# Attention over a graph's edges on one Trainium2 core: the edges' biases summed inside the keys' rows instead of added afterwards

## The chip, the core and the metric

The kernel runs on one core of one Trainium2 chip. The metric is the device time of one execution in microseconds. TensorE is called PE in what follows (its weight loads PEld), VectorE DVE, ScalarE ACT, GpSimd POOL, SyncE SP. Before the change six runs have a median of 11079.71 us (11026.39 to 11104.98).

## What is computed

Two layers of a graph network over 10,000 nodes of 512 numbers and 160,000 edges (src, dst), sorted by dst. The first layer is a mixture of four two-layer graph convolutions. The second, which the change touches, is attention along the edges with 8 heads of 64, a feed-forward part and norms:

```python
z = _layernorm(x, ln_att_g, ln_att_b)
q = (z @ Wq.T + bq).reshape(n, H, D)
k = (z @ Wk.T + bk).reshape(n, H, D)
v = (z @ Wv.T + bv).reshape(n, H, D)
s = jnp.einsum('ehd,ehd->eh', q[src], k[dst]) / np.sqrt(D) + att_bias
m = jax.ops.segment_max(s, src, num_segments=n)
p = jnp.exp(s - m[src])
denom = jax.ops.segment_sum(p, src, num_segments=n)
alpha = p / jnp.where(denom[src] == 0, 1.0, denom[src])
agg = jax.ops.segment_sum(alpha[:, :, None] * v[dst], src, num_segments=n)
att = agg.reshape(n, C) @ Wo.T + bo
x = x + att
z = _layernorm(x, ln_ff_g, ln_ff_b)
h = jax.nn.silu(z @ W1.T + b1)
x = x + h @ W2.T + b2
```

`att_bias` has 8 numbers for each edge, one for each head. They are the biases that the change moves.

## The kernel before

The work has three stages. The first two compute the first layer; at the end of the second, `nodes(b)` computes q, k and v of a block of 128 nodes and writes k and v side by side into rows of `kv_all`: 512 numbers of k, then 8 heads of 65 numbers of v, whose 65th place holds a one, so that the weighted sum of the v rows gives the denominator too (`VH` = 65, `KVW` = 512 + 520 = 1032).

The third stage is the attention with its feed-forward part. The 79 blocks of 128 source nodes are cut into windows of 32 nodes, 4 a block, 316 in all. A window's edges fill five chunks of 128 edges, one edge a partition. Four chunks are the window's own and lie in one of four buffers `kvb`; the fifth is shared by the four windows of a block and lies in one of three buffers `kvo`. POOL fetches the rows of `kv_all` by index (`fetch`, L1797), two windows ahead. Indices, places and biases of a block's edges are in a tile `meta`.

All order is written out by hand, on PE, DVE, ACT and POOL: each engine runs its instructions in the order in which the program lists them. The loop `for w in range(NW + 3)` is one window, j is its place in the block. Within it:

- `score(g)` (L2071, DVE) multiplies the queries, spread to the edges by PE (`expand`, L2034), with two chunks of keys, in place; after both, L2107 sums 64 products a head, and L2110 adds the biases from `meta`. The shared chunk goes the same way once a block, at j = 3: `expand_over` (L2042), `score_over` (L2048, L2050, L2052). Its result is copied into the window's scores by ACT at the head of the window (L2065).
- `weigh(w, s)` is a generator that three windows in a row drive on: maxima (L1936), turned by PE into a PSUM tile `turns` (L1938), the top (L1941), spread back by PE (L1943), subtracted (L1945), exp (L1948), a one-hot matrix times the weights (L1957: chunks 2 to 4 on POOL, 0 and 1 on DVE), 80 small products on PE (L1971), denominators (L1976, L1977), the scaled sums (L1980), turned (L1982) and copied into `att_t` (L1983).
- The one-hot matrices of a block's edges are made by DVE at the end of j = 1 (`open_block`, L1772, L1776, copied twice by ACT, L1778). PE turns four of them for each window two windows ahead (`turn_hots`), and the four of the shared chunk (`over_t`) at the end of j = 2; both through `turned` (L1821, L1824), whose PSUM place is in the same bank as the turned maxima.
- The feed-forward part of blocks already done is cut into small pieces. `front(b)` projects the attention's result (L1839, L1841), adds the input (L1845), norms (L1848, L1918, L1921, L1924, L1925, L1851) and turns it (L1862, L1863); `back` computes the two layers for two blocks together (L1879, Silu L1881; L1889, L1891); `tail` adds and norms the result (L1897, L1901, L1904). They are generators too. A piece that yields a positive cost is PE work and runs when credit is there; a `yield 0` puts the rest off to the next call. `advance(rate)` is called four times a window:

```python
credit[0] = min(credit[0], 0.5) + rate
for job in list(jobs):
    free = True
    while job.cost not in (None, STOP) and (
            free if job.cost == 0 else rate and credit[0] >= 0.5 * job.cost):
        free = free and job.cost > 0
```

A job thus passes at most one `yield 0` in a call. The calls are at the head of the window (rate 2.6), before the second products (0), before the next turning of one-hots (0), and before L2107 (2.4). `front(b)` is made at j = 2 of the next block, just ahead of the last of these.

Of the kernel before, what the change touches and what calls it, by code (L numbers as in the profile page):

```python
# [13 lines left out]
ALU = mybir.AluOpType  # L14
# [5 lines left out]
D = 512  # L20
# [3 lines left out]
H = 8  # L24
# [592 lines left out]
FAR = 999.0  # L617
WP = 2 + H
VH = DH + 1
KVW = D + H * VH  # L620

GROUP = 5
ROWS_OF = {1: P, 2: 2 * P, 3: 2 * P, 4: 3 * P, 5: 3 * P}
# [14 lines left out]
def fast(ctx: ExitStack, tc: tile.TileContext, a: dict, out: bass.AP, bad: bass.AP):  # L638
# [112 lines left out]
    def normed(pool, src, t):  # L751
        st = pool.tile([P, 6], F32, name="st")
        nc.vector.bn_stats(st, src)
        mv = pool.tile([P, 2], F32, name="mv")
        nc.vector.bn_aggr(mv, st)
        rs = pool.tile([P, 2], F32, name="rs")
        nc.scalar.activation(rs[:, 0:1], mv[:, 1:2], AF.Sqrt, bias=eps)
        nc.vector.reciprocal(rs[:, 0:1], rs[:, 0:1])
        nc.vector.scalar_tensor_tensor(rs[:, 1:2], mv[:, 0:1], -1.0, rs[:, 0:1],
                                       op0=ALU.mult, op1=ALU.mult)  # L760
        nc.scalar.activation(t, src, AF.Identity, scale=rs[:, 0:1], bias=rs[:, 1:2])
        return t

    mid = ExitStack()
    mp = mid.enter_context(tc.tile_pool(name="mid", bufs=1))
# [677 lines left out]
    with ExitStack() as p2:  # L1443
# [178 lines left out]
        def nodes(b):  # L1622

            xb = load_x(dp, b, 1)
            for v in range(2):
                nc.gpsimd.indirect_dma_start(
                    out=back[:, v, :], out_offset=None,
                    in_=done_s[group[b] % 3][:NE * GR[group[b]], :],
                    in_offset=row_at(pos_i[:, v, b:b + 1]),
                    bounds_check=NE * GR[group[b]] - 1, oob_is_err=False)  # L1630
            yield
            for v in range(2):
                nc.vector.scalar_tensor_tensor(xb, back[:, v, :], gsel[:, v, b:b + 1], xb,
                                               op0=ALU.mult, op1=ALU.add)
            x1 = normed(dp, xb, back[:, 0, :])
            nc.sync.dma_start(x1_all[b * P:(b + 1) * P, :], x1)
            z = normed(dp, x1, back[:, 1, :])
            yield
            pt = pt_.tile([P, KD, P], F32, name="pt")
            for k in range(KD):  # L1640
                nc.tensor.transpose(pt[:, k, :], z[:, k * P:(k + 1) * P], ident)
            z_t = dp.tile([P, KD, P], F32, name="z_t", bufs=1)
            nc.scalar.copy(z_t, pt)  # L1643
            yield
            r = slice(b * P, (b + 1) * P)
            for i in (1, 2, 0):
                po = pm.tile([P, D], F32, name="mm")
                for k in range(KD):
                    nc.tensor.matmul(po, z_t[:, k, :], wqkv[i][:, k, :], start=(k == 0),  # L1649
                                     stop=(k == KD - 1))  # L1650
                row = bias[:, NE + i, :]
                if i == 1:
                    nc.vector.tensor_add(kv[:, :D], po, row)
                elif i == 2:
                    nc.vector.tensor_add(kv[:, D:].rearrange("p (h d) -> p h d", h=H)[:, :, :DH],
                                         po.rearrange("p (h d) -> p h d", h=H),
                                         row.rearrange("p (h d) -> p h d", h=H))
                    nc.sync.dma_start(kv_all[r, :], kv)
                else:

                    q3 = dp.tile([P, 3, D], BF16, name="q3", bufs=1)
                    left = dp.tile([P, D], F32, name="left", bufs=1)
                    s = DH ** -0.5
                    nc.vector.tensor_add(left, po, row)
                    nc.scalar.activation(q3[:, 0, :], left, AF.Copy, scale=s)
                    nc.vector.scalar_tensor_tensor(left, left, s, q3[:, 0, :],
                                                   op0=ALU.mult, op1=ALU.subtract)
                    nc.scalar.copy(q3[:, 1, :], left)
                    nc.vector.tensor_sub(q3[:, 2, :], left, q3[:, 1, :])
                    nc.sync.dma_start(q_all[b].rearrange("t p d -> p t d"), q3)  # L1670
                yield
# [34 lines left out]
    with ExitStack() as p3:  # L1706
# [125 lines left out]
        def front(b):  # L1832

            x1, att_t = rest.pop(b)
            bank = yield from take()
            po = banks[bank]
            for h in range(NQ):
                yield WO
                nc.tensor.matmul(po, att_t[:, h, :, :].rearrange("p j n -> p (j n)"), wo[:, h, :],  # L1839
                                 start=(h == 0), stop=False)  # L1840
            nc.tensor.matmul(po, onesb, bias[:, 0, :], start=False, stop=True)  # L1841
            yield 0
            yield 0
            x2 = dp.tile([P, D], F32, name="x2", bufs=4)
            nc.vector.tensor_add(x2, po, x1)  # L1845
            yield 0
            st = dp.tile([P, 6], F32, name="st")
            nc.vector.bn_stats(st, x2)  # L1848
            rs, mean = yield from scale(st)
            z = dp.tile([P, D], F32, name="z")  # L1850
            nc.scalar.activation(z, x2, AF.Identity, scale=rs, bias=mean)  # L1851
            nc.gpsimd.tensor_tensor(x2, x2, x1, op=ALU.add)
            yield 0
            yield 0
            yield TURN
            i = b % 2
            if i == 0:
                pairs[b // 2] = z_ts[b // 2 % 2], []
            z_t, mine = pairs[b // 2]
            pt = po.rearrange("p (k n) -> p k n", n=P)  # L1860
            for k in range(KD):
                nc.tensor.transpose(pt[:, k, :], z[:, k * P:(k + 1) * P], ident)  # L1862
            nc.scalar.copy(z_t[:, :, i * P:(i + 1) * P], pt)  # L1863
            unused.append(bank)
            mine.append((b, x2))
            if i or b == NB - 1:
                jobs.append(Job(back(*pairs.pop(b // 2))))
# [42 lines left out]
        def take():  # L1910
            while not unused:
                yield 0
            return unused.pop(0)
# [16 lines left out]
        def weigh(w, s):  # L1930
# [35 lines left out]
            for c in range(CAP):  # L1966
                kv = kvb[w % KB][:, c, :] if c < SC_W else kvo[b % 3]
                for f in range(2):
                    for h in range(4):
                        v = D + (f * 4 + h) * VH  # L1970
                        nc.tensor.matmul(acc[h * W:(h + 1) * W, f, :], ohp[:, c, f * 4 + h, :],  # L1971
                                         kv[:, v:v + VH], start=(c == 0 and f == 0),
                                         stop=(c == CAP - 1 and f == 1), skip_group_check=True)
# [37 lines left out]
        with tc.manual_schedule(engines={ET.PE, ET.DVE, ET.Activation, ET.Pool}):  # L2011
# [32 lines left out]

            def score_over(b):
                if b < NB:
                    k = kvo[b % 3][:, :D]
                    nc.vector.tensor_tensor(k, qe.pop(b)[:, 0, :], k, op=ALU.mult)  # L2048
                    s = s_over[b] = dp.tile([P, H], F32, name="s_over")
                    nc.vector.tensor_reduce(s, k.rearrange("p (h d) -> p h d", h=H),  # L2050
                                            axis=AX.X, op=ALU.add)
                    nc.vector.tensor_add(s, s, blocks[b][0][:, SBC - 1, 2:])  # L2052

            expand_over(0)
            score_over(0)
            expand(0, 0)
            expand(0, 1)
            EARLY, LATE = 2.6, 2.4
            for w in range(NW + 3):
# [3 lines left out]
                if w < NW:  # L2063
                    s = dp.tile([P, CAP, H], F32, name="s", bufs=3)
                    nc.scalar.copy(s[:, SC_W, :], s_over[b])  # L2065

                def score(g):
                    if w < NW:
                        cs = GROUPS[g]
                        k = kv[:, cs[0]:cs[-1] + 1, :D]  # L2070
                        nc.vector.tensor_tensor(k, qe.pop((w, g)), k, op=ALU.mult)  # L2071

# [25 lines left out]
                if last:  # L2100
                    expand(w + 1, 1)
                advance(LATE)
                if j == 2 and b + 1 < NB:
                    over_t[b + 1] = turned(b + 1, range(SC_W, BC, CAP), "over_t", 2)
                first = iter(())
                if w < NW:
                    nc.vector.tensor_reduce(s[:, :SC_W, :],  # L2107
                                            kv[:, :, :D].rearrange("p c (h d) -> p c h d", h=H),
                                            axis=AX.X, op=ALU.add)
                    nc.vector.tensor_add(s[:, :SC_W, :], s[:, :SC_W, :],  # L2110
                                         blocks[b][0][:, j * SC_W:(j + 1) * SC_W, 2:])
                    first = weigh(w, s)
                    next(first)
                next(first, 1)
# [65 lines left out]
```

## Time and profile before

| | us |
|---|---|
| median of six runs | 11079.71 |
| profiled execution | 11096.67 |
| its span, first to last instruction | 11094.9 |
| PE busy over the span | 9407.8 (85%) |
| DVE busy | 5185.0 (47%) |
| ACT busy | 2975.6 (27%) |
| POOL busy | 7004.7 (63%) |
| mean granted clock of PE | 0.932 |

The averages over the span hide the stages. From 8000 to 11000 us, all of it in the third stage, PE is busy for 2615 of 3000 us, DVE for 2509, ACT for 1837 and POOL for 1966; the DMA engines' mean share is 0.76, at 243 GB/s.

A line of a group gives the source line, engine and operation, the tiles written and read, shapes and count, then busy us and mean ns of one, then the engine's idle time just before these instructions, with what ended it. A line of the timeline gives start and duration in us, and in brackets the idle time before. The chain of waits follows back, from the last instruction, what each one waited for.

### The profile page before, as it was taken

What the parts mean: (1) busy time and instruction counts of PE and PEld (TensorE: products, weight loads), DVE (VectorE), ACT (ScalarE), POOL (GpSimd) and SP (SyncE); (2) the same over time, 40 slices, a digit from 0 to 9 for tenths busy, and PEclk for the clock granted to TensorE, in tenths of its full rate; (3) what the DMA queues carried; (4) which work ended last, traced back from release to release, by engine and by line L of the source; (5) the groups of instructions that cost most, each with busy time, mean ns of one, the idle gap of its engine ahead of it and who ended that gap; (6) DMA issues with size and microseconds to landing.
All of it is one profiled execution on the core that took longest, in us unless ns stands there. A gap on an engine that the chain in (4) does not pass through costs nothing. (4 is left out here: it accounts for less than half of the span.)

```text
span 11094.9 us, 154933 instructions
## 1 busy us (share of the span) xinstructions
PE 9407.8 (85%) x56450; PEld 4520.8 (41%) x56450; DVE 5185.0 (47%) x8694; ACT 2975.6 (27%) x5619; POOL 7004.7 (63%) x6861
## 2 busy tenths in 40 slices
PE   7999999999986777887878888888788888888888
PEld 2443444333331222333333333333455555555555
DVE  5888884111130111221222222222588888888885
ACT  1110111011000111111111111112256666666665
POOL 5566676666657766666666666664366666666664
PEclk8999999999998888999889999999899999999999
DMA  8555555555546666776767777775577777777774
GB/s 253 171 163 166 161 171 168 157 161 169 157 136 208 211 217 208 241 238 222 234 222 239 241 242 239 236 229 170 174 244 248 248 243 244 247 251 246 246 243 131
DMA packets 931577, 2328.72 MB, mean 210 GB/s; under 512 B 202864, under 2 KB 288758, under 8 KB 930806
## 3 DMA queue, kind: packets, MB, share of 16 engines
q0 software_dynamic: 575968, 1787.05, 51.0%
q1 hardware_dynamic: 344864, 518.29, 14.1%
q10 hardware_dynamic: 9974, 13.39, 0.4%
q8 instruction: 449, 7.36, 0.3%
q14 instruction: 322, 2.64, 0.1%
HBM read 2047.01 MB, written 394.25 MB: 220 GB/s over the span
## 5 line engine op out<-in xcount | busy, mean ns | idle before, releaser
L1269 POOL DMA_INDIRECT ring<-in_x_dram,idx_t x1264 | 1634.9, 1293 | 887.0 <-PE p_ag L1305 466.2
L1344 PE MATMUL mm<-big,tt 128*128 128x512 f32 x4424 | 2025.5, 609 | 32.3 <-issue 17.6
L1141 POOL DMA_INDIRECT sorted<-pay,addr x1250 | 1267.2, 1014 | 381.0 <-issue 355.0
L1344 PEld LDWEIGHTS mm<-big,tt 128*128 128x128 f32 x4424 | 841.3, 195 | 1158.1 <-issue 1100.7
L1599 PE MATMUL mm<-big,turned 128*128 128x512 f32 x2688 | 1236.8, 603 | 1.4 <-issue 1.3
L1504 POOL DMA_INDIRECT ring<-h_tab,ix x747 | 763.4, 1022 | 620.1 <-PE p_ag L1539 180.9
L1797 POOL DMA_INDIRECT kv<-kv_all,meta x948 | 981.3, 1035 | 256.4 <-issue 201.8
L1649 PE MATMUL mm<-ext,z_t 128*128 128x512 f32 x1896 | 915.4, 634 | 190.4 <-ACT z_t L1643 117.1
L1348 ACT ACTIVATE y<-y 128x512 f32<-128x512 f32 x316 | 198.9, 629 | 2801.1 <-DVE y L1347 2274.3
L1504 POOL DMA_INDIRECT y<-h_tab,ix x596 | 608.6, 1021 | 510.7 <-issue 156.4
L1957 POOL TENSOR_TENSOR ohp<-oh,p 128x768 f32<-128x768 bf16 x316 | 467.0, 1478 | 694.2 <-ACT p L1948 694.2
L1539 PE MATMUL p_ag<-ring,oh 128*32 128x512 f32 x2812 | 723.7, 645 | 184.5 <-DMA ring<-h_tab,ix 141.9
L1347 DVE TENSOR_TENSOR y<-mm,bl 128x512 f32<-128x512 f32 x316 | 216.8, 688 | 1323.2 <-PE mm L1344 428.5
L1539 PE MATMUL p_ag<-y,oh 128*32 128x512 f32 x2244 | 623.4, 648 | 174.5 <-DMA y<-h_tab,ix 130.1
L1602 DVE TENSOR_TENSOR res<-mm,bias 128x512 f32<-128x512 f32 x192 | 132.7, 691 | 1332.8 <-PE mm L1599 646.8
L1879 PE MATMUL bank<-big,big 128*128 128x256 f32 (+1 forms) x2560 | 632.2, 391 | 86.2 <-ACT big L1881 78.3
L1599 PEld LDWEIGHTS mm<-big,turned 128*128 128x128 f32 x2688 | 496.6, 194 | 511.1 <-issue 510.8
L1649 PEld LDWEIGHTS mm<-ext,z_t 128*128 128x128 f32 x1896 | 376.1, 203 | 691.3 <-issue 555.5
L1578 ACT COPY turned<-pt 128x512 f32<-128x512 f32 x384 | 223.7, 584 | 1602.8 <-PE pt L1576 676.5
L1889 PE MATMUL bank<-big,big 128*128 128x512 f32 x1264 | 591.2, 598 | 1.2 <-ACT big L1863 0.7
L2071 DVE TENSOR_TENSOR kv<-qe,kv 128x1024 f32<-128x1024 f32 x474 | 575.1, 1213 | 34.1 <-DMA kv<-kv_all,meta 33.9
L1879 PEld LDWEIGHTS bank<-big,big 128*128 128x128 f32 x2560 | 481.8, 197 | 210.0 <-ACT big L1881 119.1
(383 smaller groups left out, 14955.9 us busy)
## 6 DMA issues: line engine op xcount, KB each, us to landing
h_tab<-y SPq DMA_DIRECT2D x632, 256.0 KB
means<-by_exp SPq DMA_DIRECT2D x192, 256.5 KB
done<-res SPq DMA_DIRECT2D x192, 256.0 KB
kv_all<-kvt SPq DMA_DIRECT2D x79, 516.0 KB
xb<-in_x_dram SPq DMA_DIRECT2D x156, 256.0 KB
q_all<-q SPq DMA_DIRECT2D x79, 384.0 KB
q<-q_all SPq DMA_DIRECT2D x237, 128.0 KB
ring<-in_x_dram,idx_t POOLq DMA_INDIRECT x1264
```

Of the source, the lines that this page charges most:

```text
L1141: inst = nc.gpsimd.indirect_dma_start(out=sorted1[:], out_offset=bass.IndirectOffsetOnAxis(ap=addr_i[:, c0 + c:c0 + c + 1], axis=0), in_=p ...
L1269: nc.gpsimd.indirect_dma_start(out=gbuf[i % DEEP], out_offset=None, in_=x, in_offset=bass.IndirectOffsetOnAxis(ap=source(b, k), axis=0), b ...
L1344: nc.tensor.matmul(ph, tt[:, j, k, i * P:(i + 1) * P], w[:, k, :], start=(j + k == 0), stop=(j == 1 and k == KD - 1))
L1504: nc.gpsimd.indirect_dma_start(out=ybuf[i % YB], out_offset=None, in_=h_flat, in_offset=bass.IndirectOffsetOnAxis(ap=edges[b][2][:, k:k + ...
L1539: nc.tensor.matmul(sums[b][v][j * W:(j + 1) * W, :], oh[:, j, c, :], y, start=(c == 0), stop=False, skip_group_check=True)
L1599: nc.tensor.matmul(pr, t[:, k, :], w[:, k, :], start=(i + k == 0), stop=(i == 1 and k == KD - 1))
L1649: nc.tensor.matmul(po, z_t[:, k, :], wqkv[i][:, k, :], start=(k == 0), stop=(k == KD - 1))
L1797: nc.gpsimd.indirect_dma_start(out=to, out_offset=None, in_=kv_all[:], in_offset=bass.IndirectOffsetOnAxis(ap=blocks[b][0].bitcast(I32)[:, ...
L1879: nc.tensor.matmul(ph, up(f, k), z_t[:, k, :m], start=(k == 0), stop=(k == KD - 1))
L1889: nc.tensor.matmul(po, hid[:, k, i * P:(i + 1) * P], w2[k // KD][:, k % KD, :], start=(k == 0), stop=False)
L1957: eng.tensor_tensor(ohp[:, c0:c1], oh[:, k + c0:k + c1, 0:1, :] .to_broadcast([P, n, H, W]), p[:, c0:c1, :, None].to_broadcast([P, n, H, W ...
L2071: nc.vector.tensor_tensor(k, qe.pop((w, g)), k, op=ALU.mult)
```

## The change

The keys' part of a row gets 65 places a head as well, so a row has 2 x 520 = 1040 numbers. At the head of a window ACT copies the biases from `meta` into the 65th places of the fetched keys, and once a block, at j = 3, those of the shared chunk for the next block. The products leave the 65th places alone, the sum over 65 places takes the bias in, and the two adds on DVE (L2110, L2052) go. The adds in `nodes` write the keys by heads with a gap, as they did the values. The turning of the shared one-hots, `over_t`, moves from behind the last `advance` of j = 2 to the head of j = 2. `front` has one `yield 0` more ahead of its projection and one more behind it.

```diff
-KVW = D + H * VH
+
+HV = H * VH
+KVW = 2 * HV
...
+    def by_head(t):
+        return t.rearrange("p (h d) -> p h d", h=H)[:, :, :DH]
...
                 if i == 1:
-                    nc.vector.tensor_add(kv[:, :D], po, row)
+                    nc.vector.tensor_add(by_head(kv[:, :HV]), by_head(po), by_head(row))
                 elif i == 2:
-                    nc.vector.tensor_add(kv[:, D:].rearrange("p (h d) -> p h d", h=H)[:, :, :DH],
-                                         po.rearrange("p (h d) -> p h d", h=H),
-                                         row.rearrange("p (h d) -> p h d", h=H))
+                    nc.vector.tensor_add(by_head(kv[:, HV:]), by_head(po), by_head(row))
...
             x1, att_t = rest.pop(b)
+            yield 0
             bank = yield from take()
...
             nc.tensor.matmul(po, onesb, bias[:, 0, :], start=False, stop=True)
+            yield 0
             yield 0
             yield 0
             x2 = dp.tile([P, D], F32, name="x2", bufs=4)
...
-                        v = D + (f * 4 + h) * VH
+                        v = HV + (f * 4 + h) * VH
...
-                    k = kvo[b % 3][:, :D]
-                    nc.vector.tensor_tensor(k, qe.pop(b)[:, 0, :], k, op=ALU.mult)
+                    k = kvo[b % 3][:, :HV]
+                    nc.vector.tensor_tensor(by_head(k), by_head(qe.pop(b)[:, 0, :]), by_head(k),
+                                            op=ALU.mult)
                     s = s_over[b] = dp.tile([P, H], F32, name="s_over")
                     nc.vector.tensor_reduce(s, k.rearrange("p (h d) -> p h d", h=H),
                                             axis=AX.X, op=ALU.add)
-                    nc.vector.tensor_add(s, s, blocks[b][0][:, SBC - 1, 2:])
+
+            def bias_over(b):
+
+                if b < NB:
+                    nc.scalar.copy(kvo[b % 3][:, :HV].rearrange("p (h d) -> p h d", h=H)[:, :, DH],
+                                   blocks[b][0][:, SBC - 1, 2:])
...
                     nc.scalar.copy(s[:, SC_W, :], s_over[b])
+                    nc.scalar.copy(
+                        kv[:, :, :HV].rearrange("p c (h d) -> p c h d", h=H)[:, :, :, DH],
+                        blocks[b][0][:, j * SC_W:(j + 1) * SC_W, 2:])
+                if last:
+                    bias_over(b + 1)
+                if j == 2 and b + 1 < NB:
+                    over_t[b + 1] = turned(b + 1, range(SC_W, BC, CAP), "over_t", 2)
...
-                        k = kv[:, cs[0]:cs[-1] + 1, :D]
-                        nc.vector.tensor_tensor(k, qe.pop((w, g)), k, op=ALU.mult)
+                        k = kv[:, cs[0]:cs[-1] + 1, :HV].rearrange("p c (h d) -> p c h d", h=H)
+                        k = k[:, :, :, :DH]
+                        nc.vector.tensor_tensor(
+                            k, qe.pop((w, g)).rearrange("p c (h d) -> p c h d", h=H), k,
+                            op=ALU.mult)
...
                 advance(LATE)
-                if j == 2 and b + 1 < NB:
-                    over_t[b + 1] = turned(b + 1, range(SC_W, BC, CAP), "over_t", 2)
                 first = iter(())
                 if w < NW:
                     nc.vector.tensor_reduce(s[:, :SC_W, :],
-                                            kv[:, :, :D].rearrange("p c (h d) -> p c h d", h=H),
+                                            kv[:, :, :HV].rearrange("p c (h d) -> p c h d", h=H),
                                             axis=AX.X, op=ALU.add)
-                    nc.vector.tensor_add(s[:, :SC_W, :], s[:, :SC_W, :],
-                                         blocks[b][0][:, j * SC_W:(j + 1) * SC_W, 2:])
```

More of the change, by code (lines that the diff above doesn't have):

```diff
@@ L2051, in score_over @@
                                             axis=AX.X, op=ALU.add)
-                    nc.vector.tensor_add(s, s, blocks[b][0][:, SBC - 1, 2:])
+            def bias_over(b):
+                if b < NB:
+                    nc.scalar.copy(kvo[b % 3][:, :HV].rearrange("p (h d) -> p h d", h=H)[:, :, DH],
+                                   blocks[b][0][:, SBC - 1, 2:])
             expand_over(0)
+            bias_over(0)
             score_over(0)
```

## The prediction

> **What bounds the kernel now.** I read first the windows view, to find the stage that the change touches. The attention stage runs from about 7960 to 11020 us: 316 windows in some 3060 us, 9.67 us each, a block of four windows 38.7 us. One stretch of 500 us (columns: span, then busy us of PE, PEld, DVE, ACT, POOL, then granted clock, DMA share, GB/s):
>
> ```profile
> 9500.00:10000.00 500.00, 435.27 (x5781) 285.21 (x5780) 423.57 (x717) 312.45 (x619) 331.42 (x340) 1.00 0.78 249
> ```
>
> PE is idle 64.7 of 500 us, DVE 76.4: neither is free, so I asked what PE waits for. The groups of the stage (window 7700 to 11095; idle before and who ended it stand last):
>
> ```profile
> L1879 PE MATMUL bank<-big,big 128*128 128x256 f32 x2496 | 620.8, 392 | 79.6 <-ACT big L1881 71.7 <-issue 2.6 <-ACT big L1863 0.4
> ...
> L1971 PE MATMUL sums<-kv,ohp 128*32 128x65 f32 x15168 | 374.0, 226 | 157.1 <-issue 153.8
> L1948 ACT ACT_TABLE_LOAD x268 | 343.8, 1283 | 184.2 <-DVE rs L1924 95.7 <-DVE s L1945 65.1 <-issue 13.1
> ...
> L1881 ACT ACT_TABLE_LOAD x233 | 298.9, 1283 | 4.2
> ...
> L2110 DVE TENSOR_TENSOR s<-s,meta 128x32 f32<-128x32 f32 x316 | 245.2, 776 | 10.9
> ...
> L1938 PE MATMUL turns<-ident,wide 128*128 128x128 f32 x316 | 95.0, 301 | 139.7 <-DVE den L1976 80.6 <-issue 29.1 <-ACT over_t L1824 24.2
> ```
>
> PE loses 157 us inside its long run of small products (nothing in the change touches that), 140 us before it turns the maxima (L1938), 80 us before the feed-forward's products (L1879), which wait for ACT's Silu. These three are nearly all. The line that the change deletes, L2110, is DVE's: 245 us, though its median (by source) is 0.194 us. The timeline shows why, and shows what holds L1938:
>
> ```profile
> 9512.49 2.35 DVE L2110 TENSOR_TENSOR s<-s,meta 128x32 f32<-128x32 f32 x1
> ...
> 9513.30 1.48 POOL L1957 TENSOR_TENSOR ohp<-oh,p 128x768 f32<-128x768 bf16 x1
> ...
> 9525.33 0.39 PE L1821 MATMUL turns<-identb,oh 128*96 128x128 bf16 x4
> ...
> 9525.75 0.58 ACT L1824 COPY over_t<-turns 96x512 bf16<-96x512 bf16 x1 [2.62 <-PE turns L1821]
> ...
> 9526.39 0.33 PE L1938 MATMUL turns<-ident,wide 128*128 128x128 f32 x1 [0.67 <-issue]
> ```
>
> L2110 ends at 9514.84, just after POOL's product at 9514.78: it is long where POOL's multiply overlaps it. L1938 starts as ACT's copy of over_t ends: 0.67 us lost once a block. The chain of waits tells whether DVE's 245 us lie on the path:
>
> ```profile
> 9532.95 2.18 DVE s L2107
> 9535.13 0.02 issue
> 9535.16 0.20 DVE s L2110
> ```
>
> The maxima (L1936, 0.22) and PE's L1938 follow. Where the chain runs through L2110, it is the short one. The long ones sit in windows where PE reaches L1938 later than the maxima: after the 2.35 us case they start at 9514.94, and PE turns them only at 9516.49.
>
> **The change part by part.** Windows are named j = 0 to 3 within a block; the feed-forward job has a period of two blocks, 8 windows, 39.5 periods.
>
> *1. L2110 and L2052 go.* DVE loses 245.2 us of work. On the path: only after the blocks' last window (j = 3) and the one behind it does PE wait for the maxima. There each is worth 0.19 us (L2110), and at j = 3 L2052's 0.17 us more. L2107 sums 65 places for 64: 2.273 x 65/64, 0.035 us longer. The long stalls buy nothing, and part of them moves: at j = 1 the next instruction of this kind is L1772 (meta and iota_q in), which now comes while POOL multiplies (of the other instructions of two SBUF operands, DVE's L1957 has a median of 0.681 us and a maximum of 1.346). It costs nothing on the path, since PE is later there by those 1.5 us. The Trainium skill ("SBUF — State Buffer", section "Who interferes with whom") says that a VectorE instruction with two SBUF inputs is blocked by a GpSimd instruction that reads SBUF, and that a reduction never is; by it L1772 inherits the stall, while the trace so far has L1772 at 0.761 us at most.
>
> *2. Bias copies on ACT.* 316 of 32 elements (between L2065, 8 elements, 0.200, and L1948, 40 elements, 0.236: I take 0.24) and 79 of 8 elements: 76 + 16 = 92 us of ACT work. The products (L2071) keep their length: the add by heads with a gap (L1655) and the plain one (L1653) both have a median of 0.692 us. The copy waits for all four fetches of the window, as the products do (33.9 us in 37 waits); ACT is idle 187 of the 500 us above, and L2107 needs the copy only at the window's end (L2065 at 9518.81, L2107 at 9520.12), so I take no wait, and its length where ACT is on the chain (part 3). If fetches were late, ACT's Silu behind it would be: at most those 33.9 us.
>
> *3. over_t to the head of j = 2.* The 0.67 us goes, once a block: 24.2 + 29.1 = 53 us. The four transposes (0.22 us on the chain) now stand before the products of L1879, which in every second block wait 0.66 us for Silu at that place (9516.72 to 9517.38): 39.5 x 0.22 = 9 us more gained; in the other blocks they cost what they cost before. Against it, ACT carries 0.24 + 0.58 us at the head of j = 2. PE's next write into that bank (L1943, at 9519.69) must wait for the copy: ACT's work from Silu's end is 0.51 + 1.27 + 0.20 + 0.24 + 0.58, PE's 1.99 + 0.43; I take 0.2 us, 39.5 times, 8 us lost. In the other blocks ACT's exp comes 0.5 us later, with attention's copy (L1983) behind it, for which PE's projection waits: 0.3 us, 12 us lost. No DMA is issued by the moved step; POOL's and SP's queues keep their order.
>
> *4. The extra places in front().* The first `yield 0` is used up in the same advance in which the projection ran before, so PE's order does not change. What moves is everything behind: x2's add comes one advance later, past the keys' products and past score_over. DVE no longer stands 122 us waiting for L1841, but it then waits for L2042 anyway; and the add (0.69) now lies between L2050 and L2107 where st (0.69) and mv (0.17) lay: net, with L2052 and L2110 gone, -0.19 -0.19 -0.15 +0.69 +0.035 = +0.2 us at j = 3. In every second block that delays PE (16 / 2 = 8 us lost; so the chain above, at 9532); in the others it leaves DVE for ACT at L1945 (9493.4), before these. Behind j = 3 the maxima come 0.17 us sooner: 39.5 x 0.17 = 7 us gained.
>
> *5. ACT's order.* Sqrt (L1921) moves behind Silu at j = 0, and stands next to exp. Walking the jobs through the four advances of a window gives the 268, 233 and 158 table loads that the rows show; the same walk with the change gives 268, 195, 158. 38 loads of 1.283 us, 49 us of ACT's time, go. On the path (9498.25 to 9507.48 the chain runs on ACT) Sqrt can then not start before PE's products: exp comes 0.55 us later, but z (0.83 us) has gone from before the next Silu: net 0.28 us x 39.5 = 11 us gained. The Trainium skill ("ScalarE: Activation LUTs", section "What ACT_TABLE_LOAD costs") puts a switch at 2.66 us, with a drain behind the 1.283; by it 38 fewer would be 101 us of ACT. The trace has the exp 0.01 us behind its load, so the row stands.
>
> Rows of 4160 for 4128 bytes: 0.8% of the gathered bytes, at a DMA share of 0.78, hidden. Stage 2's adds: nothing (the row pair above).
>
> **Sum:** -53 - 9 + 8 + 12 + 8 - 7 - 11 = **-52 us**. The profiled execution took 11096.67 us (span 11094.9), 17 us above the median of 11079.71; carried to the median: **11028 us**. Bounds: fast end, all 80.6 us of L1938's waits for DVE go and the three losses don't come: 11080 - 53 - 9 - 11 - 81, 10,926. Slow end, the 53 us half given back and 92 us of copies charged at ACT's share of the chain (6% of 11095 us in 3060, 22%): 11080 - 27 + 20 = 11,073.
>
> **Rivals.** (a) *The maxima come free at once* (8%): the long L2110 stalls do delay the windows behind, and L1938's 80.6 us go too: 11028 - 81 + 7, about 10,954. For: 80.6 us is the largest named wait. Against: short L2110 on the chain. (b) *Given back on ACT* (20%): copies 92 us more against 49 us less, and exp later in two windows of eight delays POOL and the fetches; time within 0.3% (33 us, about what can be told from no change), 11,080. For: ACT's Silu already holds PE 71.7 us. (c) *The products wait for the copy* (17%), the slow side: if a write into the 65th places counts as touching the same rows, L2071 at the window's head must wait for ACT. Its place: DVE, in order, with everything behind. Its price: L2071 started at 9544.22 and 9516.15, L2065 in the same windows at 9544.67 and 9518.81; the copy would end 0.45 us after that, so 0.9 to 3.1 us later. DVE's slack is 76.4 x 9.67/500 = 1.5 us a window and 0.6 more from the stalls, so it decides from about 2 us; with one of the two shown 1 us over, half of 316 windows: 158 us, 11,186. Against: the places are disjoint. That the change doesn't do what it says, the stall staying whole with L1772, is in part 1 and costs nothing while PE is later. A last 3%: slower by causes not seen, and 52% for the forecast.
>
> **How the numbers follow.** Forecast 11028, own range 10,990 to 11,073. Faster by over 0.3%: the 52% less 3 that fall short, and (a): 0.57. Within: (b) and these: 0.23. Slower: (c) and the rest: 0.20. The range reaches down to (a)'s side, 10,950, and up to 11,150, toward (c).
>
> **What would show it.** After: L1938's idle falls from 140 to about 90 us with no wait for over_t; Silu's table loads are 195; L1772 grows to some 1.5 us; L1845 waits for no PE; L2071 starts before L2065 in its window. If L2071 is released by ACT, (c) holds; if L1879's idle grows above 80 us, (b); if PE's idle for L1971 (157 us) moves, something I did not see.

## The result, and the profile after

| | before | after |
|---|---|---|
| median, us | 11078.61 (46 runs, 11024.21 to 11137.58) | 11010.61 (20 runs, 10970.68 to 11064.45) |
| ratio, 95% interval | | 0.9943 (0.9929 to 0.9957) |
| profiled execution, us | 11096.67 | 11044.7 |
| its span, us | 11094.9 | 11042.3 |
| mean granted clock of PE | 0.932 | 0.932 |

The change makes the kernel 0.57% faster, 63 us by the ratio, where 52 were forecast. All of it lies in the attention stage: from the first copy at a window's head to the last it takes 3032.0 us in the profile before (L2065) and 2966.1 in the one after (L2077). The end of the stages ahead is the same within 8 us (7958.9 and 7966.3).

The diff moves the lines: L1938, the turned maxima, is L1943 after; L1879 is L1884; L1971 is L1976; L1941 is L1946; L1772 is L1775; L1839 is L1843; L1845 is L1850; L1824 is L1827; L2071 is L2091; L2065 is L2077. L2078 is the new bias copy. The groups of the attention stage after (columns as before: busy us and mean ns, then idle before and who ended it):

```profile
L1884 PE MATMUL bank<-big,big 128*128 128x256 f32 x2496 | 613.8, 389 | 52.8 <-ACT big L1886 51.4 <-issue 0.8
...
L1976 PE MATMUL sums<-kv,ohp 128*32 128x65 f32 x15168 | 377.2, 225 | 188.0 <-issue 186.2
...
L1886 ACT ACT_TABLE_LOAD x195 | 250.2, 1283 | 4.1 <-PE bank L1884 0.6
...
L1943 PE MATMUL turns<-ident,wide 128*128 128x128 f32 x316 | 90.7, 287 | 93.6 <-DVE den L1981 86.4 <-DVE wide L1941 3.5 <-ACT oh_t L1827 2.9
L1946 DVE TENSOR_REDUCE top<-turns 128x1 f32<-128x128 f32 x316 | 90.6, 287 | 131.5 <-ACT over_t L1827 101.5 <-PE turns L1943 20.5 <-ACT kv L2078 7.5
...
L2078 ACT COPY kv<-meta 128x32 f32<-128x32 f32 x237 | 59.9, 253 | 183.7 <-DMA kv<-kv_all,meta 149.3 <-issue 34.1
...
L1775 DVE TENSOR_TENSOR oh<-meta,iota_q 128x512 bf16<-128x512 f32 x79 | 55.5, 703 | 0.0
...
L1850 DVE TENSOR_TENSOR x<-bank,x 128x512 f32<-128x512 f32 x79 | 54.0, 684 | 4.8 <-PE bank L1845 4.8
...
L1981 DVE TENSOR_SCALAR den<-sums 128x2 f32<-128x2 f32 x316 | 48.0, 152 | 181.2 <-ACT att_t L1988 178.6 <-issue 2.4
```

Two of these groups as they were before:

```profile
L1941 DVE TENSOR_REDUCE top<-turns 128x1 f32<-128x128 f32 x316 | 89.3, 283 | 9.7 <-PE turns L1938 9.5
...
L1845 DVE TENSOR_TENSOR x<-bank,x 128x512 f32<-128x512 f32 x79 | 54.7, 692 | 127.2 <-PE bank L1841 102.3 <-issue 24.9
```

PE's idle before the maxima falls from 139.7 to 93.6 us, and no part of what is left waits for `over_t`; PE's idle before the feed-forward's products, most of it for Silu, falls from 79.6 to 52.8 us; Silu loads its table 195 times for 233. Against it, PE's stalls in the sums grow from 157.1 to 188.0 us. Two waits are new. ACT stands 183.7 us at its bias copies, mostly until fetches land, and DVE stands 101.5 us before the top (L1946) until ACT has copied `over_t`. The timeline shows how that second one comes about, at the head of j = 2 (start, duration, and idle before in brackets):

```profile
9476.87 0.27 PE L1943 MATMUL turns<-ident,wide 128*128 128x128 f32 x1
...
9476.98 0.39 PE L1824 MATMUL turns<-identb,oh 128*96 128x128 bf16 x4
...
9477.19 0.69 DVE L1962 TENSOR_TENSOR ohp<-oh,p 128x512 f32<-128x512 bf16 x1
...
9478.04 1.26 ACT L1781 COPY oh<-oh 128x1280 bf16<-128x1280 bf16 x1
...
9479.41 0.59 ACT L1827 COPY over_t<-turns 96x512 bf16<-96x512 bf16 x1
...
9480.03 0.29 DVE L1946 TENSOR_REDUCE top<-turns 128x1 f32<-128x128 f32 x1 [2.15 <-ACT over_t L1827]
9480.24 1.22 DVE L2091 TENSOR_TENSOR kv<-qe,kv 128x1024 f32<-128x1024 f32 x1
```

PE has turned the maxima (9476.87) and then the shared one-hots (9476.98) into one PSUM bank. DVE could reduce the maxima from 9477.88 on; it starts when ACT, with a copy of 1.26 us in front, has taken the one-hots out (9480.00). The next products stand behind it. The Trainium skill ("PSUM — Partial Sum Buffer", section "PSUM bank collisions raise a hardware error") asks that two engines be kept apart by the bank, even where both only read and at other addresses; the wait is what keeping to that costs here, and only the trace says how much.

### The profile page after: what moved, and what is told of

Read it like the earlier page. It is cut to its first block, busy times and chain, and to the rows that moved or that the text cites. A ratio compares the mean times of both kernels' runs of the same rounds, so it can differ in the third digit from the quotient of the medians.

```text
span 11042.3 us, 155394 instructions
## 1 busy us (share of the span) xinstructions
PE 9383.7 (85%) x56450; PEld 4494.2 (41%) x56450; DVE 4938.0 (45%) x8299; ACT 2965.4 (27%) x5976; POOL 7008.4 (63%) x6861
## 5 line engine op out<-in xcount | busy, mean ns | idle before, releaser
L1884 PE MATMUL bank<-big,big 128*128 128x256 f32 (+1 forms) x2560 | 627.1, 389 | 59.3 <-ACT big L1886 57.8
L2091 DVE TENSOR_TENSOR kv<-qe,kv 128x1024 f32<-128x1024 f32 x474 | 575.5, 1214 | 68.0 <-DMA kv<-kv_all,meta 61.9
L2127 DVE TENSOR_REDUCE s<-kv 128x32 f32<-128x2080 f32 x237 | 547.7, 2311 | 0.0
```

The source lines that it names most:

```text
L1884: nc.tensor.matmul(ph, up(f, k), z_t[:, k, :m], start=(k == 0), stop=(k == KD - 1))
L2091: nc.vector.tensor_tensor(k, qe.pop((w, g)).rearrange("p c (h d) -> p c h d", h=H), k, op=ALU.mult)
L2127: nc.vector.tensor_reduce(s[:, :SC_W, :], kv[:, :, :HV].rearrange("p c (h d) -> p c h d", h=H), axis=AX.X, op=ALU.add)
```

## The experiments

Twelve runs were made in three groups, each on another chip than the other groups and timed against the kernel before on the same chip. Their medians of the kernel before tell the chips apart: 10497.63 us in the first group, 10495.01 in the second, 11027.54 in the third, against 11078.61 where the result was measured (the record names no chip for the result; its median sets it apart from the first two groups).

### First group: the parts alone

**One-hots alone.** The kernel before with this edit:

```diff
                     nc.scalar.copy(s[:, SC_W, :], s_over[b])
+                if j == 2 and b + 1 < NB:
+                    over_t[b + 1] = turned(b + 1, range(SC_W, BC, CAP), "over_t", 2)
...
                 advance(LATE)
-                if j == 2 and b + 1 < NB:
-                    over_t[b + 1] = turned(b + 1, range(SC_W, BC, CAP), "over_t", 2)
```

> The kernel before, with the turning of the shared one-hots at the head of j = 2 and nothing else. Theory A (the gain is the 0.67 us that PE lost once a block behind the copy of over_t): 0.4 to 0.6% faster, some 11,020 to 11,035 us, and PE's idle before the turned maxima falls from 140 to about 86 us with no wait for over_t. Theory B (the gain is DVE's freed 245 us): within 0.15% of before. Theory C (the gain is ACT's 38 table loads): within 0.15% of before.

Measured: 10446.98 us, ratio 0.9952 (0.9938 to 0.9965). The groups:

```profile
L1938 PE MATMUL turns<-ident,wide 128*128 128x128 f32 x316 | 94.2, 298 | 159.0 <-DVE den L1976 135.4 <-ACT oh_t L1824 18.5 <-DVE wide L1936 4.6
L1941 DVE TENSOR_REDUCE top<-turns 128x1 f32<-128x128 f32 x316 | 90.2, 286 | 24.3 <-ACT over_t L1824 24.3
```

No wait for `over_t` is left at L1938; DVE's new one is 24.3 us here. 0.48% is 50 us: this part alone makes about what the sum gave the wait (53), and more than the 42 that the sum left of it after the terms beside it (-9, +8, +12).

**Places alone.** The kernel before with the two extra places:

```diff
             x1, att_t = rest.pop(b)
+            yield 0
             bank = yield from take()
...
+            yield 0
             yield 0
             yield 0
             x2 = dp.tile([P, D], F32, name="x2", bufs=4)
```

> The kernel before, with the two extra places in front() and nothing else. Silu's table loads fall from 233 to 195 in every theory. Theory A: within 0.2%, since the add of x2 now lies on DVE's path at j = 3 and takes back what ACT gains. Theory C: 0.3 to 0.5% faster, the 49 us of loads or more. Theory B: within 0.15%.

Measured: 10538.02 us, 1.0044 (1.003 to 1.0057), slower than any of the three theories had it. First two groups, then a timeline of its window j = 3:

```profile
L1940 PE MATMUL turns<-ident,wide 128*128 128x128 f32 x316 | 97.8, 309 | 308.1 <-DVE den L1978 248.4 <-ACT over_t L1824 52.3 <-DVE wide L1938 4.1
...
L1847 DVE TENSOR_TENSOR x<-bank,x 128x512 f32<-128x512 f32 x79 | 54.0, 684 | 4.8 <-PE bank L1842 4.8
```

```profile
9259.88 0.19 DVE L1947 TENSOR_TENSOR s<-s,turns 128x40 f32<-128x40 f32 x1
9259.98 0.69 DVE L1847 TENSOR_TENSOR x<-bank,x 128x512 f32<-128x512 f32 x1
...
9260.70 0.69 DVE L1850 BATCH_NORM_STATS2 st<-x 128x6 f32<-128x512 f32 x1
...
9261.57 2.28 DVE L2109 TENSOR_REDUCE s<-kv 128x32 f32<-128x2048 f32 x1
...
9264.11 0.22 DVE L1938 TENSOR_REDUCE wide<-s 128x8 f32<-128x40 f32 x1
...
9264.48 0.30 PE L1940 MATMUL turns<-ident,wide 128*128 128x128 f32 x1 [1.74 <-DVE den L1978]
```

x2's add (L1847) waits for PE only 4.8 us in all, but it stands with the norm's first step between the weights and the sum (L2109), and PE waits 1.74 us for the maxima behind them. By the mean distances of the heads' copies, the j = 3 windows of the two blocks of a period take 10.42 and 10.50 us, for 9.67 and 10.08 in the kernel before (its profile is in the second group): 1.17 us, 39.5 times, 46 us. The window j = 0 that saves a table load gives back 0.71 us, 28 us in all; the other five take 0.35 us together, 14 us. That is 32 us of the 40 that the times show.

**Biases alone.** The changed kernel without the extra places and with `over_t` at its old place; so the adds on DVE are gone and ACT copies the biases.

> The kernel before, with the biases in the 65th places (copies on ACT at the head of the window, both adds gone), the shared one-hots still turned at the end of j = 2 and no extra places. Theory B: 0.3 to 0.6% faster. Theory A: within 0.2%, and PE's idle before the turned maxima still about 130 us or more, with the wait for over_t in it. ACT's new copies wait some 100 to 180 us for fetches in either.

Measured: 10500.1 us, 1.0002 (0.9993 to 1.0011). The groups (L1941 is the turned maxima here, L2076 the bias copies):

```profile
L1941 PE MATMUL turns<-ident,wide 128*128 128x128 f32 x316 | 95.1, 301 | 142.5 <-DVE den L1979 77.4 <-ACT over_t L1827 52.4 <-ACT oh_t L1827 10.1
...
L2076 ACT COPY kv<-meta 128x32 f32<-128x32 f32 x237 | 59.2, 250 | 254.5 <-DMA kv<-kv_all,meta 224.6 <-issue 29.4
```

DVE's share of the idle before the turned maxima is 77.4 us, for 145.0 in the kernel before (second group): that is what taking the adds off DVE buys. But ACT's copies stand 254.5 us, 224.6 of them for fetches (100 to 180 were expected), and PE's idle before the feed-forward's products is 129.3 us (103.1 in the kernel before, second group). In the time gain and loss cancel; that it is these waits that cancel is a reading, not a measurement.

**One-hots and places together**, the first two edits.

> The kernel before, with the moved one-hots and the extra places, the biases still added on DVE. Theory A: 0.4 to 0.7% faster, as much as the whole change or more, since the bias part gains nothing. Theory B: at most half of the whole change's 0.57%.

Measured: 10488.88 us, 0.9992 (0.9983 to 1.0001). Against the one-hots alone on the same chip the places cost 42 us (10446.98 to 10488.88), against the kernel before 40 (10497.63 to 10538.02): the two parts add. Theory A's 0.4 to 0.7% did not come. The result is below half of the whole change's 0.57%, as B had it, but the gain that B looks for in the biases did not show in them alone either.

### Second group: the whole, and the whole without one part

**The changed kernel** itself:

> The changed kernel once more, beside its parts. So far on this chip: one-hots alone -0.48%, extra places alone +0.44%, biases alone 0.02%, one-hots and places together -0.08%. If the parts add up: between -0.1 and +0.1%. If the biases' part pays for the places (DVE's path at j = 3 gets the add of x2, and only without L2110 and L2052 has room for it): 0.4 to 0.7% faster, as measured first.

Measured: 10514.08 us, 1.0021 (1.0012 to 1.003). On this chip the change makes the kernel slower. Its groups:

```profile
L2091 DVE TENSOR_TENSOR kv<-qe,kv 128x1024 f32<-128x1024 f32 x474 | 576.4, 1216 | 268.6 <-DMA kv<-kv_all,meta 267.7 <-issue 0.2
...
L1976 PE MATMUL sums<-kv,ohp 128*32 128x65 f32 x15168 | 273.1, 225 | 0.0
...
L1775 DVE TENSOR_TENSOR oh<-meta,iota_q 128x512 bf16<-128x512 f32 x79 | 180.0, 2278 | 0.0
...
L1943 PE MATMUL turns<-ident,wide 128*128 128x128 f32 x316 | 91.3, 289 | 152.8 <-DVE den L1981 146.7 <-ACT oh_t L1827 2.7 <-DVE wide L1941 2.6
...
L2078 ACT COPY kv<-meta 128x32 f32<-128x32 f32 x237 | 59.2, 250 | 410.1 <-DMA kv<-kv_all,meta 378.4 <-issue 31.0
```

The sums (L1976) have no stall at all here, for 188 us on the chip of the result. The bias copies wait more than twice as long, and the products, too, wait for fetches.

**The kernel before, profiled on that chip** (no edit):

> The kernel before, for its profile on the chip of these runs. If the stalls of PE inside the long run of small products (157 us, ended by issue) belong to the kernel: some 150 us again. If to the first chip: near 0, as in the four runs so far.

Measured: 10491.53 us, one run. The groups:

```profile
L1971 PE MATMUL sums<-kv,ohp 128*32 128x65 f32 x15168 | 274.3, 226 | 0.0
...
L1938 PE MATMUL turns<-ident,wide 128*128 128x128 f32 x316 | 98.8, 313 | 222.4 <-DVE den L1976 145.0 <-ACT over_t L1824 52.4 <-ACT oh_t L1824 18.0
...
L1772 DVE TENSOR_TENSOR oh<-meta,iota_q 128x512 bf16<-128x512 f32 x79 | 63.2, 800 | 0.0
```

The stalls belong to the chip, not to the change: 0 us here, 157.1 in the first profile of the same kernel. So do the waits at L1938: 222.4 us for 139.7. The wait that the prediction put at 53 us is 52.4 here, whole under its own name.

**Without the places** (one-hots and biases):

> The changed kernel without the two extra places in front(): moved one-hots and biases in the rows. If the parts add up: 0.4 to 0.55% faster. If the biases' part gains only together with the places: the same, so this run alone decides nothing, but Silu's table loads are 233 again and PE's idle before the feed-forward's products (L1879 of before) is above 100 us. ACT's bias copies at the head, waiting for fetches, could make it worse: down to -0.2%.

Measured: 10486.08 us, 0.9989 (0.998 to 0.9998), 28 us below the changed kernel: not the 0.4 to 0.55% of parts that add up. Beside the one-hots alone, each against the kernel before on its own chip, the biases take 0.37% back; the copies stand 379.6 us here.

**Without the move of `over_t`** (biases and places):

> The changed kernel with the shared one-hots turned at the end of j = 2 again: biases and places. If the parts add up: 0.3 to 0.5% slower than before. If the biases' part pays for the places: within 0.2% of before or up to 0.3% faster, with PE's waits for DVE before the turned maxima well below the 248 us of the places alone.

Measured: 10529.26 us, 1.0035 (1.0021 to 1.0048); PE waits 52.4 us for `over_t` again. This is what parts that add up would give. It is 0.14% above the changed kernel, and the two intervals overlap: beside the biases and the places the move brings less than alone.

### Third group: other places, and a slower PE

This chip has the stalls in the sums again.

**One-hots and biases, with the copies later.** The changed kernel without the places, and:

```diff
                     nc.scalar.copy(s[:, SC_W, :], s_over[b])
-                    nc.scalar.copy(
-                        kv[:, :, :HV].rearrange("p c (h d) -> p c h d", h=H)[:, :, :, DH],
-                        blocks[b][0][:, j * SC_W:(j + 1) * SC_W, 2:])
...
+                if w < NW:
+                    nc.scalar.copy(
+                        kv[:, :, :HV].rearrange("p c (h d) -> p c h d", h=H)[:, :, :, DH],
+                        blocks[b][0][:, j * SC_W:(j + 1) * SC_W, 2:])
                 next(one, 1)
                 if w >= 2:
```

> The shared one-hots at the head of j = 2 and the biases in the 65th places, without the extra places in front(); and the bias copies moved from the head of the window to just ahead of the exp. If the copies cost because they stand at the window's head and wait there for fetches, with ACT's Silu and attention's copy behind them, then most of the bias step's cost goes: ACT's idle before the copies falls from 380 us (copies at the head) to under 60, the products still wait for fetches, and the ratio is 0.992 to 0.996, that is at or below 0.9952 (the one-hots alone). If the copies cost by their own 76 us of ACT work, or DVE gained nothing by the adds' going, the ratio stays near 0.9989 (the same kernel with the copies at the head).

Measured: 10948.51 us, 0.9927 (0.9904 to 0.995). The groups:

```profile
L1941 PE MATMUL turns<-ident,wide 128*128 128x128 f32 x316 | 89.7, 284 | 50.7 <-DVE den L1979 43.9 <-ACT oh_t L1827 3.2 <-DVE wide L1939 2.6
...
L2109 ACT COPY kv<-meta 128x32 f32<-128x32 f32 x237 | 56.1, 237 | 69.8 <-DMA kv<-kv_all,meta 69.8
```

The copies stand 69.8 us, a little over the 60 expected. This chip's PE is the slower kind, so the nearest comparison of that wait is the changed kernel's 183.7 on the chip of the result, not the 380 of the second group. No run on this chip has the copies at the head and nothing else different (with the places and 20 more products, below, they stand 69.5 us there), so what the later place is worth isn't shown.

**One-hots behind the turned maxima**, at the end of j = 2, and nothing else:

```diff
                 advance(LATE)
-                if j == 2 and b + 1 < NB:
-                    over_t[b + 1] = turned(b + 1, range(SC_W, BC, CAP), "over_t", 2)
...
                 next(first, 1)
+                if j == 2 and b + 1 < NB:
+                    over_t[b + 1] = turned(b + 1, range(SC_W, BC, CAP), "over_t", 2)
                 next(two, 1)
```

> The kernel before with only the shared one-hots moved, and not to the head of j = 2 but behind the turned maxima of the same window, at its end. If all that counts is that PE turns the maxima without waiting for the copy of over_t, the gain is that of the move to the head: the idle before L1938 has no wait for over_t and the ratio is 0.994 to 0.997. If the four turnings at the head of j = 2 were worth something of their own (hidden in a wait for Silu), less comes: 0.997 to 0.999. If the copy behind delays the top or the weights of the window instead, the wait comes back under L1943 or L1941, and the ratio is 0.999 to 1.002.

Measured: 10933.72 us, 0.9918 (0.9888 to 0.9948). The groups:

```profile
L1938 PE MATMUL turns<-ident,wide 128*128 128x128 f32 x316 | 91.0, 288 | 84.5 <-DVE den L1976 76.1 <-DVE wide L1936 3.9 <-ACT oh_t L1824 3.8
...
L1941 DVE TENSOR_REDUCE top<-turns 128x1 f32<-128x128 f32 x316 | 89.3, 283 | 5.1 <-PE turns L1938 4.5 <-ACT over_t L1824 0.6
```

PE's wait for `over_t` is gone, and DVE's does not appear (0.6 us for 101.5). Two moved lines, without places or biases, do within the intervals as much on this chip as the whole change did on the one of the result. The gain is larger than the 0.994 to 0.997 expected, though the interval reaches into it. What the four turnings hide at the head of j = 2 was not needed for that; the move to the head was not run by itself on this chip.

**A longer sums run, before and after.** The edit in the kernel before (the changed kernel has HV for D):

```diff
+            for i in range(20):
+                h = i & 3
+                nc.tensor.matmul(acc[h * W:(h + 1) * W, 0, :], ohp[:, 0, h, :],
+                                 kvb[w % KB][:, 0, D + h * VH:D + h * VH + VH], start=True,
+                                 stop=(i >= 16), skip_group_check=True)
             for c in range(CAP):
```

> The kernel before with 20 products more ahead of each window's 80 (repeats of the first four, overwritten by the real ones): on the chips of the other experiments PE has no stall in that run, on the chip of the first result it stalls 0.5 us a window there. 20 of them at 24 ns are 0.49 us a window, 154 us in all, so this puts such a loss back by hand. If PE's path sets the pace everywhere, 1.013 to 1.015. If the other engines have as much to say, 1.004 to 1.012.

Measured: 11115.23 us, 1.0081 (1.0061 to 1.0101), some 89 us. More than 154 us were put in: a window's 80 are matmul instructions, two for each of the kernel's 40 products, so 20 products are 40 instructions, 12,640 in all. From the first of them to the first real one the trace has 0.59 us a window (median), some 187 us. About half comes through, so the other engines have as much to say as PE. And the changed kernel with it:

> The changed kernel with the same 20 products. If the sign of the change depends on whether PE loses time in that run (then ACT, DVE and the fetches have slack for the copies and for x2's add), this is below the kernel before with the 20 products, by 20 to 66 us (0.2 to 0.6%). If the sign depends on something else of the first chip, it stays above by some 20 us (0.2%), as without the 20 products.

Measured: 11109.68 us, 1.0063 (1.0042 to 1.0084). The two lie 5.6 us apart and their intervals overlap: neither 20 us below nor 20 above, inconclusive. Groups of the second (L2083 is the bias copy, L1981 the real sums):

```profile
L1981 PE MATMUL sums<-kv,ohp 128*32 128x65 f32 x15168 | 346.1, 231 | 177.1 <-issue 176.7
...
L1943 PE MATMUL turns<-ident,wide 128*128 128x128 f32 x316 | 89.7, 284 | 48.1 <-DVE den L1986 30.9 <-issue 10.5 <-DVE wide L1941 2.6
...
L2083 ACT COPY kv<-meta 128x32 f32<-128x32 f32 x237 | 60.2, 254 | 69.5 <-DMA kv<-kv_all,meta 46.3 <-issue 23.0
```

The slack came as the theory has it: the copies' wait for fetches is the less, the more PE is held up, 378.4 us on the second chip, 149.3 on that of the result, 46.3 here. The time did not follow.

## Why the prediction was right, and where it was not

The time (11028 forecast, 11010.61 measured) and the direction were right, and so, as far as the runs show, was the term that carries them. Two other terms were mis-sized.

**The move of `over_t`** (-53). Right: no wait for `over_t` before the maxima, and alone 50 us on the first chip. A price was set at 8 us, for PE's write behind ACT's copy. The one who waits is DVE, whose top reads the same bank: 101.5 us, where L1941 stood 9.7 before (24.3 with the move alone on the first chip). How much of that reached the end was not measured by itself; the placement behind the maxima shows that it need not be paid.

**The extra places** (+8 - 7 - 11 with the table loads). The facts were right: 195 loads, and L1850 waits 4.8 us for PE where it waited 102.3. The sum was not. Alone they cost 40 us, with the one-hots 42 (both on the first chip), in the whole change 28 (on the second), where the three terms give -10 us. The step that failed is the charge of x2's add to the path at j = 3: +0.2 us net, and only in every second block, with the adds' going set against it. Without the adds' going its own terms give 0.54 us (0.69 - 0.15). Measured with the places alone, the j = 3 windows are 0.75 and 0.42 us longer: about that, but in both blocks of the period. So the 38 loads saved don't pay for it on those two chips; on the chip of the result it was not run.

**The bias copies** (92 us of work, no wait). The work was right: 0.253 us each. The wait failed: "at most those 33.9 us" was read from what the products waited for before. But the copy stands at the window's head, earlier than the products on DVE, and waits for all fetches: 149.3 us, 224.6 to 378.4 on chips with a faster PE, with ACT's Silu behind it. The gain was missed too: with only the biases moved, PE's waits for DVE before the maxima are 77.4 us for 145.0, on chips without the stalls. Alone the two cancel (1.0002). With the one-hots moved they cost 0.37% at the window's head, and no cost can be told at the later place (0.9927 beside 0.9918); but the later place was run on another kind of chip, so it is not shown that the place makes the difference.

**The stalls of L2110.** That they buy nothing was not shown by itself: the biases alone bring nothing, but the copies' waits are in that sum. That L1772 grows to some 1.5 us was too little on one kind of chip and too much on the other. It takes 2.0 to 2.3 us in the four kernels of the first two groups without the adds, where den (L1981) hardly waits (4 to 31 us); in the changed kernel there POOL's multiply overlaps it 76 times of 79. It takes 0.70 us in the profile of the result, with 2 overlaps of 79, and as much in the third group's two kernels without the adds. On the chip of the result ACT's `att_t` holds den for 181.2 us in all, and with it L1775 behind it: at 9473.61 POOL's multiply starts, at 9475.10 it ends, and L1775 starts at 9475.25. So the rule of the Trainium skill cited in the prediction ("SBUF — State Buffer", section "Who interferes with whom") shows where the two instructions overlap, as in the 2278 ns above, and has nothing to say where they don't. (With the places and the adds both there, L1772 takes 1.25 and 1.36 us, overlapped 16 and 19 times, so the adds' going is not the only thing that brings the two together.)

**The rivals.** (a) fell where the result was measured: of the 80.6 us that L1938 waited for DVE, none went (86.4 after). On the chips without stalls the biases alone took nearly half of that wait away, and the time stayed. (c) fell in every profile: the products of keys wait for fetches and PE, never for ACT's copy. (b), given back on ACT, did not decide where the result was measured: PE's idle before those products fell by 27 us, with 38 loads fewer. On the second chip copies wait 378.4 us ahead of Silu and the change loses, but PE's idle before those products falls there too (103.1 to 85.0 us), so the loss does not show where (b) put it.

**The sums' stalls**, said to be untouched, grew by 31 us. The six profiles of kernels with the stalls show 139 to 191 us at the window's own keys. They are least where 20 products were put ahead of the kernel before, and larger after the change than before it, with those 20 products (139.2 to 177.1 us) and without, in one profile each: it reads as if part of what PE gains elsewhere were lost here. Why was not tested.

**What stays open.** Why the whole change gains 0.57% on one chip and loses 0.21% on another. The parts were not run on the chip of the result; with two terms mis-sized elsewhere, that the sum came within 11 us of the gain there is luck as far as the runs show. Without stalls the parts give -0.48, +0.44 and 0.0%, the whole measured +0.21. All the pairs were run there too, and one pair does not add: one-hots and biases give -0.11% where their sum is -0.46. The 0.35% between them is of the size of what the whole is off by (0.25). The trace has a reading for it: in the j = 3 windows the copies wait 214 us with the biases alone and 346 with the one-hots moved as well, when the j = 2 windows ahead are shorter.

The same windows part the chips. By the mean distances of the heads' copies, the windows j = 0 and 1 of a period become shorter in all by 0.84 us on the chip of the result and by 1.05 on the second; those of j = 2 and 3 become shorter by 0.79 us on the first of these and longer by 1.44 on the second. Over 39.5 periods that is 88 us, where the whole stage differs by 79 (65.9 gained, 12.7 lost). At j = 3 the copies wait 134 us on the chip of the result and 360 on the second. So the fetches for j = 3 are the place to look; no run moved them. The attempt to bring the gain back by a longer PE run was inconclusive.

## What to carry to other kernels

Price a wait by what shares the bank, on every engine that reads or writes it: moving a copy out of one engine's way put it in another's. Work put on an idle engine stands there waiting for what isn't ready at its new place, with all that is queued behind it, so look at what it waits for and not only at its length; whether a place just ahead of its reader is better is open here. And a change of several parts is worth taking apart: here two moved lines gain by themselves on both kinds of chip, and on the chips without stalls a part that cuts 38 table loads loses more than it saves by putting an add ahead of the maxima.

## What was not expected of the hardware

The same program takes 11,079 us where the result was measured, 11,028 on the third group's chip and 10,495 to 10,498 on two others. Most of that lies ahead of the attention stage, in stages that nothing here looked into: in the two profiles of the kernel before, the stage starts at 7958.9 us on the chip of the result and at 7455.7 on the second, and takes 3032.0 and 2930.6 us. In the attention stage the slower ones stall before the small products of L1971, 157.1 us in one profile; the others not once in eight profiles. The granted clock in that stage was close (0.97 on the chip of the result and 0.99 on the second, both for the kernel before), and one of these products takes 226 ns in both.

The stalls keep to one place: of the 336 that are longer than 0.1 us in the first profile, 288 stand before the 41st to 50th of a window's 80 matmuls. They are hardly waits for instructions. One DMA queue of instructions moved 449 packets of 16 KB in both profiles, and 548 with the 20 products more, so it is PE's: PE's 112,900 instructions (matmuls and loads) are 251 a packet. But a packet was under way in only 16% of those stalls, and the last one had landed 6.6 us (median) before the stall ended. What they wait for stays open. The sign of a change of half a per cent came out differently on two chips.
